# Sixteen products and their additions moved ahead of the edges in the last two row tiles of a four-layer graph kernel

## The chip, the cores and the metric

The kernel runs on one core of one Trainium2 chip. The metric is the device time of one execution in microseconds (us). The time before is the median of three runs, 1643.59 us (1642.99 to 1648.46).

The core has five engines that work side by side and wait for each other through semaphores: TensorE (PE, matrix products), VectorE (DVE), ScalarE (ACT), GpSimd (POOL) and SyncE (SP, which here only issues DMAs). SBUF is the on-chip memory, PSUM the small memory that TensorE writes its products to.

## What is computed

The input is a node matrix x of 4096 x 128 and a sparse weighted matrix adj of 4096 x 4096, both float32. Four graph layers follow each other, and each is a residual step with a layer norm:

```python
x = layernorm(x + L0(x, adj, W, a))        # signed attention
x = layernorm(x + L1(x, adj, W0, W1))      # Chebyshev convolution
x = layernorm(x + L2(x, adj, weight, ...)) # four attention heads
x = layernorm(x + L3(x, adj, W_self, W_neigh))

# L2: attention of each node over its entries of adj
C = alpha_src[None, :, :] + alpha_dst[:, None, :]
tau = adj.T[..., None] * exp(maximum(0.2 * C, C))
z = einsum('mnh,nhf->mhf', adj.T[..., None] * tau / tau.sum(1, keepdims=True), h_prime)

# L3: mean over neighbours
deg = clip(adj.sum(1, keepdims=True), 1.0)
out = h @ W_self + (adj @ h / deg) @ W_neigh
```

The change concerns the end of the kernel, where L2 and L3 run interleaved.

## The kernel before

The 4096 nodes are cut into 32 row tiles of 128 (t = 0 to 31) and into 8 column blocks of 512. In L2, adj is treated as a list: each node has a few non-zero entries, and for each row tile the rows of a table in device memory that these entries name are gathered by GpSimd's indirect DMAs, nine per tile (`gathers`, L1846). L3 treats adj as a dense matrix and streams its columns from device memory in chunks of 1 MB (`columns`, L1945, issued on SP's queue). Both are done in one loop over the row tiles (L2109 to L2134), so that a row tile that L2 has finished can enter L3 at once.

The order of the work on TensorE, VectorE, ScalarE and GpSimd is the order in which the program writes it (`manual_schedule`, L2009): no scheduler moves anything. What can be said early and done late is therefore written out by hand with two queues of generators. `pieces` holds L3's products, `chains` the steps that turn a finished row tile into L3's input. The steps of one row tile t in the loop are:

- `targets(t + 1)` (L1861): three small matmuls on TensorE for the next tile.
- `multiply(6)`: up to six products of L3. One product (L1957) is a matmul of 128 x 128 y by a 128 x 512 piece of the chunk; the products of one column block over the row tiles of a group add up in one PSUM bank of the pool "pp", which has four. When the last product of a block is written, the bank goes on the list `adds`. `multiply` stops as soon as four banks are on it.
- `edges(t)` (L1872 to L1884): the attention weights of L2, on VectorE, with one exponential on ScalarE (L1879). It needs the gathered rows.
- `add_up()` (L1970): VectorE adds every bank on `adds` to the running sum acc3 in SBUF, and so frees the banks.
- `sums` (L1889, L1890): four matmuls that add up the weighted rows. They need the results of `edges`.
- `multiply(2)`: two more products.
- `divide` (L1896 to L1898) and `turn` (L1907): the row tile is divided by its weights' sum, added to x and transposed on TensorE.
- When a group of row tiles is complete, `layer3_rows` (L1914 to L1933): ScalarE copies the transposed tile, TensorE multiplies it by L3's two weight matrices (L1924), and ScalarE scales the result to y (L1928) and to x (L1933). From then on the group's products are on `pieces`. Between its three steps stand single products.
- `gathers(t + 2)`: GpSimd's gathers for the tile after the next.

The groups have 1, 1, 2, 4, 4, 4, 4, 2, 2, 2, 2, 2, 1 and 1 row tiles. The last three are 28 and 29 together, 30, and 31. When t = 30 begins, the products of 28 and 29 (16 of them) are still to be done, and a few of the group before.

After the loop (L2135 to L2139) what is left on `pieces` is done, two products at a time with their additions. The products of row tile 31 are not on `pieces`: `layer3_end` (L1980, L1982) computes them while it transposes acc3 block by block, divides by the degree, normalizes (L1984 to L2006) and writes the output (L2007). The first L1982 needs y of row tile 31.

The core of the two helpers that the change calls:

```python
def multiply(n):
    for _ in range(n):
        if len(adds) > 3:
            break
        one(pieces)
```

Of the kernel before, what the change touches and what calls it, by code (L numbers as in the profile page):

```python
# [47 lines left out]
def adj_resnorm_d4(ctx: ExitStack, tc: tile.TileContext, x_in, xT_in, adj, adjT, pairs, diag_in, w0g, w0gT, a0, w1a, b1a,  # L48
# [9 lines left out]
    NT = N // P  # L58
# [623 lines left out]
    def network(usual):  # L682

        with ExitStack() as whole:
# [161 lines left out]
            if usual:  # L846
                sparse_layers(enter, lists, w, h0T)
                return
# [885 lines left out]
    def sparse_layers(enter, lists, w, h0T):  # L1734
# [103 lines left out]
        def gathers(t, behind={}):  # L1838
            if t >= NT:
                return  # L1840
            if t not in got:
                got[t] = l2.tile([P, E, F + H], F32, name="got", bufs=4)
            if 2 <= t < EARLY:
                nc.scalar.copy(got[t][:, 0:QT, :], packed[:, t - 2])
            for j in range(QT if t < EARLY else 0, E):
                nc.gpsimd.indirect_dma_start(got[t][:, j, :], None, table,  # L1846
                                             bass.IndirectOffsetOnAxis(ap=lists.source[:, t, j:j + 1], axis=0))
                if j % 2:
                    lists.pause(behind.get(j))

        def load_spread(c):
            if c < NB:
                wide[c] = l2.tile([P, TB, SLOTS], BF16, name="spread")
                nc.scalar.dma_start(wide[c].rearrange("p k s -> p (k s)"), spread[c])

        def targets(t):
            if t < NT:
                at = wide[t // TB][:, t % TB]
                told[t] = psum.tile([P, QT * W + E * H + F + H], F32, name="u")
                for j in range(QT):  # L1860
                    nc.tensor.matmul(told[t][:, j * W:(j + 1) * W], at[:, j * P:(j + 1) * P], dst[:, t], start=True, stop=True)  # L1861

        def edges(t):

            g, u = got.pop(t), told.pop(t)
            d = u[:, 0:QT * W].rearrange("p (j s) -> p j s", s=W)
            wt = u[:, QT * W:QT * W + E * H].rearrange("p (j h) -> p j h", h=H)
            a = lists.value[:, t][:, :, None].to_broadcast([P, E, H])
            gw = l2.tile([P, E + 1, F + H], F32, name="gw")
            nc.scalar.copy(gw[:, E, :], own[:, t, :])  # L1870
            into = l2.tile([P, QT, P], F32, name="into")
            nc.vector.tensor_tensor(into, lists.iota[:, None, :].to_broadcast([P, QT, P]),  # L1872
                                    d[:, :, 3 * H:W].to_broadcast([P, QT, P]), ALU.is_equal)
            e = l2.tile([P, E, H], F32, name="score")
            nc.vector.tensor_reduce(e[:, 0:QT], d[:, :, 0:3 * H].rearrange("p j (s h) -> p j h s", s=3), AX.X, ALU.add)
            nc.vector.tensor_tensor(e[:, QT:], g[:, QT:, F:F + H], near[:, t, :][:, None, :].to_broadcast([P, NEAR, H]), ALU.add)
            nc.vector.tensor_tensor(e[:, 0:QT], e[:, 0:QT], g[:, 0:QT, F:F + H], ALU.add)
            nc.vector.scalar_tensor_tensor(e, e, ALPHA, e, op0=ALU.mult, op1=ALU.max)
            nc.scalar.activation(e, e, AF.Exp)  # L1879
            nc.vector.tensor_tensor(gw[:, 0:E, F:F + H], e, a, ALU.mult)  # L1880
            nc.vector.tensor_tensor(wt, gw[:, 0:E, F:F + H], a, ALU.mult)
            nc.vector.tensor_tensor(heads(gw[:, 0:E, 0:F]), heads(g[:, :, 0:F]), wt[:, :, :, None].to_broadcast([P, E, H, FO]), ALU.mult)  # L1882
            here = l2.tile([P, F + H], F32, name="here")
            nc.vector.tensor_reduce(here, gw[:, QT:, :].rearrange("p j f -> p f j"), AX.X, ALU.add)  # L1884
            return u[:, QT * W + E * H:], into, gw, here

        def sums(so, into, gw, here):
            for j in range(QT):
                nc.tensor.matmul(so, into[:, j, :], gw[:, j, :], start=j == 0, stop=False)  # L1889
            nc.tensor.matmul(so, ident, here, start=False, stop=True)  # L1890
            return so

        def divide(t, so):
            rd = small.tile([P, H], F32, name="rd", bufs=3)
            z = l2.tile([P, 1, F], F32, name="z")
            nc.vector.reciprocal(rd, so[:, F:F + H])  # L1896
            nc.vector.tensor_tensor(heads(z), heads(so[:, None, 0:F]), rd[:, None, :, None].to_broadcast([P, 1, H, FO]), ALU.mult)
            nc.vector.tensor_add(x[:, t, :], z[:, 0, :], x[:, t, :])  # L1898
            return rd[:, 0:1]
# [3 lines left out]
        def turn(t, t0, n):  # L1903

            if t == t0:
                turned[t0] = ps_x.tile([P, n, P], F32, name="px")
            nc.tensor.transpose(turned[t0][:, t - t0, :], x[:, t, :], ident)  # L1907
            stats(x[:, t, :], t)

        def layer3_rows(t0, n):  # L1910

            s = small.tile([P, n], F32, name="rstd2")
            xb = l2.tile([P, n, P], F32, name="oT")
            nc.scalar.copy(xb, turned.pop(t0))  # L1914
            inverse(s, mv[:, t0:t0 + n, 1])
            nc.scalar.activation(warm, eps, AF.Exp)
            yield
            qs = []
            for k0 in range(0, n, 2):
                m = min(2, n - k0)  # L1920
                q = ps_x.tile([P, m, 2, F], F32, name="px")
                qs += [(k0 + k, q[:, k]) for k in range(m)]
                for k in range(m):
                    nc.tensor.matmul(q[:, k].rearrange("p s f -> p (s f)"), xb[:, k0 + k, :],  # L1924
                                     W3.rearrange("p s f -> p (s f)"), start=True, stop=True)
            yield
            for k, q in qs:
                nc.scalar.activation(y[:, t0 + k, 0:F - 1], q[:, 0, 0:F - 1], AF.Copy, scale=s[:, k:k + 1])  # L1928
            if t0 + n < NT:
                pieces.append(layer3_product(t0, n))  # L1930
                yield
            for k, q in qs:
                nc.scalar.activation(x[:, t0 + k, :], q[:, 1, :], AF.Copy, scale=s[:, k:k + 1])  # L1933
            yield
# [27 lines left out]
        def add_up():  # L1962
            while adds:
                t0, p, blk = adds.popleft()
                nonlocal summed
                summed = acc3[:, blk.start:blk.start + 1]
                if t0 == 0:
                    nc.scalar.copy(acc3[:, blk], p)
                else:
                    nc.vector.tensor_add(acc3[:, blk], p, acc3[:, blk])  # L1970
# [38 lines left out]
        with tc.manual_schedule(engines={mybir.EngineType.PE, mybir.EngineType.DVE, mybir.EngineType.Activation,  # L2009
# [3 lines left out]
            def one(queue, n=1):  # L2013
                while queue and n:
                    r = next(queue[0], queue)
                    if r is not queue:
                        n -= 1
                    else:
                        queue.popleft()
# [6 lines that stand above are left out]
# [83 lines left out]
            for t in range(NT):  # L2109
                t0, n = of[t]  # L2110
                if t % TB == 1:
                    load_spread(t // TB + 1)
                if t == 3:
                    lists.check(ps_x, "px")
                targets(t + 1)
                multiply(6)
                made = edges(t)
                add_up()
                one(chains)
                if t == t0 + n - 1:  # L2120
                    nc.scalar.activation(warm, eps, AF.Sqrt)
                so = sums(*made)
                multiply(2)
                rd = divide(t, so)
                turn(t, t0, n)
                if t == t0 + n - 1:
                    chains.append(layer3_rows(t0, n))
                for _ in range(3):
                    one(chains)
                    multiply(1)  # L2130
                behind = {1: rd}
                if summed is not None:
                    behind[5] = summed
                gathers(t + 2, behind)  # L2134
# [53 lines left out]
```

## Time and profile before

| | |
|---|---|
| Median of three runs | 1643.59 us (1642.99 to 1648.46) |
| Profiled execution | 1824.21 us, span from first to last instruction 1822.3 us |
| TensorE busy | 1538.9 us, 84% of the span |
| VectorE busy | 1140.9 us, 63% |
| GpSimd busy | 834.8 us, 46% |
| ScalarE busy | 387.1 us, 21% |
| 1755.23 to 1778.65 us of the span | TensorE busy 19.16 of 23.42, VectorE 15.95, ScalarE 8.28, GpSimd 4.87 |
| 1778.65 to 1791.53 us | TensorE busy 12.88 of 12.88, VectorE 7.72, ScalarE 1.39 |
| 1791.53 to 1822.3 us | TensorE busy 14.45 of 30.77, VectorE 18.80, ScalarE 18.09 |

The profile is of one execution with the hardware's profiler on, and that execution took 180.6 us longer than the median of the runs without it. Times of single events below are microseconds from the start of its span. In a timeline line the columns are: start, length, engine, line of the kernel, operation, what is written and read, shape, and the number of instructions merged into the line; a bracket at the end gives the idle time of the engine just before and what ended it ("issue" or "remote" where the profile shows nothing that ended it). A float32 product of L1957 appears as two matmul records. The ends of matmul records are modelled.

### The profile page before, as it was taken

How to read it: one execution, taken by the hardware profiler on the slowest of the kernel's cores; microseconds unless marked ns; L12 is line 12 of the kernel's file. 1: busy time of each engine (PE TensorE's matmuls, PEld its weight loads, DVE VectorE, ACT ScalarE, POOL GpSimd, SP SyncE). 2: the span in 40 equal slices, each digit the busy share in tenths (PEclk: the TensorE clock that was granted, in tenths of full speed). 3: DMA queues.
4: the chain of work that ended last, by engine and by line, in shares of the span. 5: the costliest groups of instructions: out<-in, count | busy, mean ns of one | idle time of the engine just before them, and what ended most of it. 6: DMA issues, size and time to landing. Idle time of an engine off the chain costs nothing.

```text
span 1822.3 us, 16500 instructions
## 1 busy us (share of the span) xinstructions
PE 1538.9 (84%) x4740; PEld 735.8 (40%) x4744; DVE 1140.9 (63%) x3209; ACT 387.1 (21%) x698; POOL 834.8 (46%) x1336
## 2 busy tenths in 40 slices
PE   6899999999999679887988968889936678878786
PEld 3344445444444224443444433444413334434334
DVE  5887647898878458764788920255426654545566
ACT  5766411100000101210200000023314111112224
POOL 0000000002423883364376784888485766766741
PEclk9899999999999779898999977999967788778988
DMA  9787675688898346563676836788864466556764
GB/s 383 290 311 263 235 259 193 245 320 307 294 340 305 115 164 237 185 222 137 206 265 220 298 95 226 264 278 286 286 165 127 162 220 226 195 194 219 223 178 110
DMA packets 111199, 421.47 MB, mean 231 GB/s; under 512 B 21685, under 2 KB 48314, under 8 KB 71290
## 3 DMA queue, kind: packets, MB, share of 16 engines
q1 hardware_dynamic: 59984, 360.01, 54.6%
q0 software_dynamic: 22656, 36.17, 8.0%
q10 hardware_dynamic: 28458, 24.14, 4.6%
q8 instruction: 39, 0.64, 0.1%
q14 instruction: 62, 0.51, 0.1%
HBM read 404.39 MB, written 15.86 MB: 231 GB/s over the span
## 4 chain that ended last, share of the span: by engine, by line
PE 49%; DVE 25%; issue 9%; another core or an unknown queue 8%; ACT 4%; DMA 3%; POOL 2%; ACTq 0%; DVEq 0%; POOLq 0%
PE pacc L731 17%; PE pacc L424 11%; PE pp L1957 6%; PE pp L2076 5%; DVE at L1403 2%; DVE top L1402 2%; DVE here L1884 2%; DVE here L1562 2%; DVE gw L1882 1%; DVE spread L1318 1%; DVE same L1318 1%; DVE acc L1970 1%; PE pden L412 1%; PE px L1924 1%
## 5 line engine op out<-in xcount | busy, mean ns | idle before, releaser
L1846 POOL DMA_INDIRECT got<-table,source x267 | 255.7, 958 | 69.3 <-issue 66.2
L1957 PE MATMUL pp<-chunk,xT 128*128 128x512 f32 x496 | 260.3, 668 | 8.1 <-ACT xT L1928 5.3
L1524 POOL DMA_INDIRECT got<-rows,source x180 | 182.7, 1015 | 123.6 <-DVE rec L1318 48.2
L731 PE MATMUL pacc<-chunk,x 128*128 128x512 f32 x512 | 222.7, 593 | 0.0
L731 PE MATMUL pacc<-chunk,t 128*128 128x512 f32 x384 | 187.9, 637 | 10.5 <-issue 10.5
L424 PE MATMUL pacc<-chunk,hw 128*128 128x512 f32 x408 | 190.7, 612 | 0.8 <-DVE hw L467 0.7
L2076 PE MATMUL pp<-chunk,w 128*128 128x512 f32 x384 | 172.1, 598 | 0.0
L731 PE MATMUL pacc<-chunk,v 128*128 128x512 f32 x320 | 154.5, 626 | 9.4 <-issue 9.3
L1360 POOL IOTA i<- 128x384 int32 (+3 forms) x4 | 0.9, 237 | 347.8 <-PE pden L412 330.7
L731 PEld LDWEIGHTS pacc<-chunk,x 128*128 128x128 f32 x512 | 96.1, 190 | 114.6 <-issue 114.6
L1957 PEld LDWEIGHTS pp<-chunk,xT 128*128 128x128 f32 x496 | 99.6, 215 | 104.9 <-issue 92.8
L1402 DVE MAX8 top<-chunk 128x8 f32<-128x512 f32 x196 | 128.5, 677 | 16.0 <-DMA chunk<-in_adjT 16.0
L1403 DVE FIND_INDEX8 at<-top,chunk 128x8 uint16<-128x512 f32 x196 | 133.1, 685 | 0.0
L731 PEld LDWEIGHTS pacc<-chunk,t 128*128 128x128 f32 x384 | 77.0, 206 | 104.1 <-issue 104.1
L1569 POOL TENSOR_TENSOR idle<-idle 128x1 f32<-128x1 f32 x508 | 114.1, 225 | 8.9
L1524 POOL DMA_INDIRECT both_ways<-in_pairs,both_at x108 | 105.3, 975 | 17.4 <-issue 17.3
L424 PEld LDWEIGHTS pacc<-chunk,hw 128*128 128x128 f32 x408 | 75.5, 193 | 92.8 <-issue 87.0
L396 ACT ACTIVATE junk<-chunk 128x2048 fp8e4<-128x2048 f32 x51 | 97.4, 1910 | 29.0 <-DMA chunk<-in_adjT 28.6
L2076 PEld LDWEIGHTS pp<-chunk,w 128*128 128x128 f32 x384 | 71.5, 193 | 78.5 <-issue 77.8
L330 DVE TENSOR_SCALAR pos<-chunk 128x2048 bf16<-128x2048 f32 x66 | 80.2, 1219 | 35.9 <-DMA chunk<-in_adjT 35.9
L1970 DVE TENSOR_TENSOR acc<-pp,acc 128x512 f32<-128x512 f32 x96 | 62.5, 683 | 61.2 <-remote 40.0
L731 PEld LDWEIGHTS pacc<-chunk,v 128*128 128x128 f32 x320 | 60.6, 198 | 83.5 <-issue 83.5
(433 smaller groups left out, 2063.6 us busy)
## 6 DMA issues: line engine op xcount, KB each, us to landing
chunk<-in_adjT SPq DMA_DIRECT2D x326, 1024.0 KB
keep<-in_adjT SPq DMA_DIRECT2D x13, 1024.0 KB
spread<-spread ACTq DMA_DIRECT2D x16, 384.0 KB
got<-table,source POOLq DMA_INDIRECT x267
chunk<-in_adjT ACTq DMA_DIRECT2D x4, 1024.0 KB
got<-rows,source POOLq DMA_INDIRECT x180
table<-rows ACTq DMA_DIRECT2D x8, 264.0 KB
xT<-in_xT ACTq DMA_DIRECT2D x8, 256.0 KB
```

Source lines behind the costliest of these rows:

```text
L330: r = nc.vector.tensor_scalar(pos, a, 0.0, None, op0=ALU.is_gt)
L396: nc.scalar.activation(junk, a, AF.Relu, scale=-1.0, accum_out=bad[:, n:n + 1], saturate=False)
L424: in_order(nc.tensor.matmul(p, hw[:, j * TB + k, :], a[:, k, :], start=first and k == 0, stop=last and k == TB - 1))
L731: nc.tensor.matmul(p, stationary(c * TB + k), a[:, k, :], start=n == 0 and k == 0, stop=n == NB - 1 and k == TB - 1)
L1402: pin(nc.vector.max(self.top[:, t, ib, :], row))
L1403: pin(nc.vector.max_index(self.at[:, t - TB, ib, :], self.top[:, t, ib, :], row))
L1524: tc.keep_in_program_order(nc.gpsimd.indirect_dma_start(out, None, of, bass.IndirectOffsetOnAxis(ap=index, axis=0)))
L1569: return nc.gpsimd.tensor_tensor(self.idle[:, 0:1], of, self.idle[:, 1:2], ALU.mult)
L1846: nc.gpsimd.indirect_dma_start(got[t][:, j, :], None, table, bass.IndirectOffsetOnAxis(ap=lists.source[:, t, j:j + 1], axis=0))
L1957: nc.tensor.matmul(p, y[:, t0 + k, :], a[:, ib % (TB // n), k, :], start=k == 0, stop=k == n - 1)
L1970: nc.vector.tensor_add(acc3[:, blk], p, acc3[:, blk])
L2076: nc.tensor.matmul(p, w[:, c * TB + k, :], a[:, k, :], start=n == 0 and k == 0, stop=n == NB - 1 and k == TB - 1)
```

## The change

In the iterations t = 30 and t = 31, after `multiply(6)` and ahead of `edges(t)`, the kernel now adds up the banks, does up to eight products, adds up, does up to eight products, and adds up. Nothing else is touched: the same products and additions are done in the same sequence among themselves. What they follow and precede on TensorE and VectorE is different.

```diff
                 targets(t + 1)
                 multiply(6)
+                if t >= NT - 2:
+                    for _ in range(2):
+                        add_up()
+                        multiply(8)
+                    add_up()
                 made = edges(t)
                 add_up()
                 one(chains)
```

`multiply(8)` stops at four full banks. A product of the group of 28 and 29 fills half a bank's sum, so eight of them fill four banks. A product of t = 30 alone completes one.

## The prediction

> **What bounds the kernel now.** The edit touches only the last two row tiles (t = 30 and t = 31) of the last loop, so I read the end of the kernel: the chain of waits in order of time, then the timelines of TensorE, VectorE and ScalarE from 1735 us on. The chain's columns are start, length, and what ran.
>
> ```profile
> 1754.12 4.33 issue
> 1758.45 0.62 ACT xT L1928 x2
> ...
> 1761.29 1.82 DVE here L1884
> ...
> 1763.96 3.56 PE pp L1957 x4
> ...
> 1778.82 12.87 PE pp L1957 x30
> ```
>
> The last stall before the close is ScalarE's 4.33 us ahead of L1928 (it makes y of row tiles 28 and 29). Then edges, sums and products alternate, and from 1778.82 to 1791.7 TensorE alone sets the time: fifteen products (two records each) that had been left over. These are what the edit moves forward.
>
> TensorE's timeline:
>
> ```profile
> 1752.46 1.13 PE L1924 MATMUL px<-W,oT 128*128 128x256 f32 x4 [1.19 <-issue]
> ...
> 1755.23 2.82 PE L1957 MATMUL pp<-chunk,xT 128*128 128x512 f32 x6
> 1761.31 1.69 PE L1889 MATMUL u<-gw,into 128*128 128x132 f32 x6 [3.26 <-issue]
> ...
> 1763.76 3.77 PE L1957 MATMUL pp<-chunk,xT 128*128 128x512 f32 x4
> 1767.33 0.31 PE L1907 MATMUL px<-ident,x 128*128 128x128 f32 x1
> ...
> 1773.06 0.84 PE L1889 MATMUL u<-gw,into 128*128 128x132 f32 x6
> ...
> 1778.65 13.04 PE L1957 MATMUL pp<-chunk,xT 128*128 128x512 f32 x30
> ```
>
> Between 1755.23 and 1791.53 TensorE idles 4.3 us (busy 19.16 of the first 23.42 us, then all of 12.88), nearly all in two places: 3.26 us ahead of the sums of t = 30, and 0.64 us before a turn. The fifteen products at the end run back to back at 0.858 us each (12.87 / 15).
>
> VectorE's timeline:
>
> ```profile
> 1740.99 0.52 DVE L1872 TENSOR_TENSOR into<-iota,u 128x384 f32<-128x384 f32 x1
> ...
> 1744.21 1.82 DVE L1884 TENSOR_REDUCE here<-gw 128x132 f32<-128x924 f32 x1
> ...
> 1759.43 0.20 DVE L1880 TENSOR_TENSOR gw<-score,value 128x36 f32<-128x36 f32 x1 [5.63 <-ACT score L1879]
> ...
> 1763.02 2.47 DVE L1970 TENSOR_TENSOR acc<-pp,acc 128x512 f32<-128x512 f32 x4
> ```
>
> An undisturbed edges step (t = 29, first two lines) takes 5.04 us from the start of L1872 to the end of L1884. That of t = 30 is broken by a wait of 5.63 us for ScalarE.
>
> **What the Trainium skill says.** "TensorE: Matmul & The Clock Gate", Part 1, "What's actually happening": after an idle window of about 3.4 us the array runs at half rate, until about 3.4 us of activity. The trace agrees: after the 3.26 us idle two products took 3.77 us, and the two after t = 31's sums, with no such idle, 1.98. The same page, Part 3, "The mechanism": matmuls start and end in program order; Part 1, "Architectural detail", says strict first-in first-out for VectorE and ScalarE. So what is put ahead really holds what follows. "Perfetto Trace Analysis", "Tensor Engine Instruction (MATMUL, LD_WEIGHTS)": a matmul's recorded end is an estimate, and others are told only when PSUM has acknowledged. Here that gap is large: L1924 ends by record at 1753.6, but L1928, which waits for it, starts at 1758.45; a column load on SP's queue that waits for the product recorded to end near 1756.3 was issued at 1763.4.
>
> **The change, part by part.** Counts are read from the built programs' order. Nothing is added or removed: the same 29 products from here to the end, the same additions, DMAs and transposes. What moves: ahead of the sums of t = 30 stand 19 products instead of 3, and ahead of its edges on VectorE 12 additions, of which 4 stood just after them and 8 come from later. Between L1924 of tile 30 and the sums of t = 31 stand 8 products instead of 5, and ahead of the edges of t = 31 9 additions that stood after them. None is left after t = 31, so the 12.87 us at the end go. SP keeps its order of column loads; five chunk buffers rotate, each load waits for the products that free its buffer, and those come earlier now. The gathers on POOL were issued for t = 31 in the iteration of t = 29 (last one at 1760.08), so they pass nothing that moved.
>
> What the move breaks is the overlap. In the kernel before, VectorE does edges while TensorE does products. Now the products of t = 30 come first, with VectorE idle apart from additions, and then the edges, with TensorE idle. The new path, from 1755.23, when the three old products start:
>
> 1. 19 products x 0.858 = 16.3.
> 2. The last addition, 0.69 + 0.03 = 0.7. Only then do t = 30's edges start.
> 3. Edges, 5.04. The 5.63 us wait for ScalarE is gone, as L1928 has run long before.
> 4. From the end of L1884 over the sums, divide and two products to the turn L1907: 4.2 as at t = 30 before (1763.11 to 1767.33) with the slow clock; 2.0 with the fast one. I count 2.0 here and the rest under "slow clock".
> 5. Turn to y of tile 30: 1767.33 to 1769.90 before, 2.6 (a table load of 1.28 is in it).
> 6. Its 8 products x 0.858 = 6.9. They read that y, so they cannot start earlier.
> 7. The last addition 0.7, then t = 31's edges 5.0.
> 8. Sums, divide, turn 1.7; turn to y of tile 31 2.6. The closing matmuls L1982 need this y. Before, it was ready at 1779.8 and hidden under the fifteen products; with that cover gone it counts.
>
> Sum 16.3 + 0.7 + 5.0 + 2.0 + 2.6 + 6.9 + 5.7 + 4.3 = 43.5 us, against 36.3 before (1755.23 to 1791.53, the first L1980): **+7.2 us**.
>
> Then three terms whose size the trace does not give for the new order:
>
> - Slow clock after idle. TensorE now idles 5 us ahead of each sums step. Ahead of t = 30's: 4.2 - 2.0 = 2.2. Ahead of the close: eight 128-column matmuls of a block took 1.9 us, at half rate 3.8, and part of the second block is slow too: 0 to 4. I take 2.2 + 2.
> - Late completions. Additions 2 to 4 of t = 30 must see their products before products reuse the four "pp" banks. If they become visible only at 1763.4, as they did before, the fifth new product starts at 1764.2 in place of 1761.5: 0 to 2.9. I take 1.5.
> - Column loads: the new order needs four 1 MB chunks in 13.7 us. Three had been issued by 1751.4, the fourth by 1763.4 for use at about 1770; cost 0, up to 3 if it lands late. Below nothing none of these terms goes, since each only adds waiting.
>
> Total 7.2 + 2.2 + 2 + 1.5 = 12.9 us. It is a difference inside the profiled execution, which took 1824.21 us (span 1822.3), while the median run is 1643.59, 11% less. The instructions at the end are of fixed length, so I carry microseconds over, not percent: 1643.6 + 12.9 = **1656.5 us**.
>
> **The rivals.**
>
> *The stalls of before belong to the profiled execution.* If completions come promptly in the timed runs, the kernel before needs only TensorE's own time in that stretch: 24.9 for products and about 4.2 for two tiles' sums, turns and L1924, 29.1 in place of 36.3. The new path, serial anyway, keeps 43.5 + 4.2. Then the change costs 18.6: about 1662. For it: the profiled execution is 180 us longer. Against it: the waits recur in every group of two tiles (at 1729.99 too), and POOL's pace would then hold the kernel before back.
>
> *The moved work fills a wait for gathers, and the kernel is not slower.* One place: L1876, where edges wait for the gathered rows of t = 30 and t = 31. POOL issues one gather per 1.3 us (seven from 1751.94 to 1761.05), so 11.7 us per tile; VectorE needs about 9.2 (edges 5.0, four additions 2.5, divide and statistics 1.7). If the timed runs are bound by POOL, edges of t = 31 wait about 4 us and those of t = 30 about 2.5, in which the moved products are free. It decides once the two waits together exceed the 12.9. Then the kernel would be at 1643 or, with 5 us more of waiting, 1638. Against it: in the last two tiles the trace has no wait for a gather at all; the longest near the end is 2.51 us, at t = 26, and POOL itself waits 4.2 us in every second tile for VectorE.
>
> *TensorE's clock stays up and completions are prompt only in the new kernel.* Then only 7.2 is left: 1650.8, still slower.
>
> **How the numbers follow.** A difference of 0.3%, 4.9 us, is about what a measurement of this kernel can tell. The forecast, serial path with 7 to 16 us, gets 0.72 (the third case is its lower end); prompt completions in the timed runs, 16 to 21 us, 0.14; gathers that hide it 0.14, half of it within 0.3% and half faster. Slower is 0.72 + 0.14 = 0.86. The range goes from 1649.5, under the third case, to 1663, over the first rival; it leaves out the gathers' case, and little above. The likeliest case's own range is 1650.5 to 1660.
>
> **What would show it.** In the changed kernel's timeline: 38 product records in one run before t = 30's sums, then TensorE idle for 4 to 5 us ahead of L1889 of t = 30 and again of t = 31; a turn of tile 31 followed directly by L1980 and L1982, with no product between; VectorE's L1872 of t = 30 right after the twelfth addition. The wait at L1880 of t = 30 falls from 5.63 us to about 0.3. From the first product of t = 30 to the first L1984 it should take 48 to 52 us in place of 38.3. I am wrong if edges of t = 30 or t = 31 wait for gathers by more than 5 us in either kernel's timed execution, if TensorE stays busy through the edges, or if the close starts within 38 us of the first product.

## The result and the profile after

The changed kernel takes 1656.95 us (median of six runs, 1654.58 to 1659.92). In the same group of runs the kernel before takes 1647.0 us (six runs, 1642.99 to 1650.0). The ratio is 1.0066, with a 95% interval from 1.0046 to 1.0086: slower by 10.0 us, between 7.6 and 14.2. The forecast was 1656.5 us, made from 1643.6 plus 12.9.

In one of the four groups of runs (`no_last_add`, `warm`, `overlap_28` and `overlap_all` below) the kernel before itself took 1830.81 us, 11% longer than in the others and like the execution behind the profile shown ahead of the prediction; times of that group are compared only within it.

The traces below set the change against a second profile of the unchanged kernel, from an execution of 1647.67 us; it is the experiment `before_again`. First the busy time by stretch: from the first product of t = 30 to the first L1984, and from there to the end. The columns are the stretch, its length, the busy time with the number of instructions of TensorE, of its weight loads, of VectorE, ScalarE and GpSimd, then TensorE's granted clock, DMA share and GB/s. The changed kernel:

```profile
1576.08:1626.49 50.41, 38.22 (x102) 19.45 (x101) 24.91 (x49) 9.06 (x21) 8.38 (x12) 0.83 0.54 129
1626.49:1655.30 28.81, 12.47 (x112) 12.28 (x110) 18.07 (x116) 18.09 (x73) 4.76 (x8) 0.78 0.25 77
```

The kernel before, the same two stretches:

```profile
1578.51:1616.99 38.48, 33.66 (x102) 17.32 (x101) 24.91 (x49) 8.96 (x21) 8.39 (x12) 0.91 0.70 170
1616.99:1645.90 28.91, 12.47 (x112) 12.28 (x110) 18.08 (x116) 18.09 (x73) 4.76 (x8) 0.75 0.25 77
```

All of the loss lies in the first stretch, 50.41 against 38.48 us, or 11.9 us; the close is the same to 0.1 us. Instruction counts are equal (102 on TensorE, 49 on VectorE), and VectorE is busy for the same 24.91 us. TensorE does the same work in 4.6 us more (38.22 against 33.66, at a lower mean clock) and idles for 12.2 us in place of 4.8. That 11.9 in the traces is 10.0 between the medians is within the scatter: the six runs of each kernel spread over 5.3 and 7.0 us, and ahead of this stretch, where both programs have the same order of instructions, the two executions differ by 2.4 us (1576.08 against 1578.51).

The chain of waits of the changed kernel (start, length, what ran), which in the kernel before ended in thirty product records, now goes over edges and sums to the end:

```profile
1585.08 8.21 DMA got<-table,source
1593.29 0.53 DVE into L1872
...
1596.52 1.82 DVE here L1884
...
1604.63 8.85 PE pp L1957 x16
...
1617.35 1.83 DVE here L1884
```

The first of these lines misleads: the chain puts the start of the edges of t = 30 down to a gather. The one issued at 1585.08 is the last of all, so it belongs to t = 31, whose edges come 20 us later, and VectorE's timeline further below shows that it reaches L1872 without idling. TensorE's timeline of the changed kernel:

```profile
1576.08 16.55 PE L1957 MATMUL pp<-chunk,xT 128*128 128x512 f32 x38
1596.54 1.69 PE L1889 MATMUL u<-gw,into 128*128 128x132 f32 x6 [3.90 <-DVE gw L1882]
...
1604.63 8.83 PE L1957 MATMUL pp<-chunk,xT 128*128 128x512 f32 x16 [1.26 <-ACT xT L1928]
1617.37 0.94 PE L1889 MATMUL u<-gw,into 128*128 128x132 f32 x6 [3.91 <-DVE gw L1882]
...
1623.81 0.79 PE L1982 MATMUL pp<-xT,chunk 128*128 128x128 f32 x2 [0.31 <-ACT xT L1928]
```

Thirty-eight records run without a break, then TensorE waits 3.90 us for edges; sixteen records, then 3.91 us for edges again. VectorE's timeline of the changed kernel shows why the edges are late:

```profile
1592.67 0.69 DVE L1970 TENSOR_TENSOR acc<-pp,acc 128x512 f32<-128x512 f32 x1 [1.02 <-PE pp L1957]
1593.28 0.54 DVE L1872 TENSOR_TENSOR into<-iota,u 128x384 f32<-128x384 f32 x1
...
1613.50 0.69 DVE L1970 TENSOR_TENSOR acc<-pp,acc 128x512 f32<-128x512 f32 x1 [0.17 <-PE pp L1957]
1614.11 0.54 DVE L1872 TENSOR_TENSOR into<-iota,u 128x384 f32<-128x384 f32 x1
```

L1872 of t = 30 starts right behind the twelfth addition, which waited for the nineteenth product. That is 17.20 us after the first product (1593.28 - 1576.08). The next line of t = 30 that needs gathered rows, L1876, starts at 1593.85 without a wait. The edges of t = 31 in the same way start behind the last addition of tile 30's products.

### The profile page after: what moved, and what is told of

Read it like the earlier page. It is cut to its first block, busy times and chain, and to the rows that moved or that the text cites. A ratio compares the mean times of both kernels' runs of the same rounds, so it can differ in the third digit from the quotient of the medians.

```text
span 1655.3 us, 16507 instructions
## 1 busy us (share of the span) xinstructions
PE 1478.9 (89%) x4740; PEld 715.9 (43%) x4744; DVE 1139.1 (69%) x3209; ACT 387.8 (23%) x698; POOL 837.0 (51%) x1336
## 4 chain that ended last, share of the span: by engine, by line
PE 42%; DVE 26%; POOL 15%; DMA 7%; issue 6%; ACT 3%; ACTq 0%; DVEq 0%; POOLq 0%
PE pacc L731 15%; PE pacc L424 12%; POOL got L1846 6%; POOL got L1524 4%; PE pp L1957 3%; PE pp L2076 3%; DMA got<-table,source 3%; DVE at L1403 3%; DVE top L1402 3%; POOL idle L1569 2%; DVE gw L1882 1%; DVE here L1884 1%; POOL value L1524 1%; DVE same L1318 1%; DVE here L1562 1%
## 5 line engine op out<-in xcount | busy, mean ns | idle before, releaser
L1957 PE MATMUL pp<-chunk,xT 128*128 128x512 f32 x496 | 244.2, 636 | 2.2 <-ACT xT L1928 2.0
L731 PE MATMUL pacc<-chunk,t 128*128 128x512 f32 x384 | 171.3, 597 | 0.0
L731 PE MATMUL pacc<-chunk,v 128*128 128x512 f32 x320 | 144.5, 597 | 0.0
L1957 PEld LDWEIGHTS pp<-chunk,xT 128*128 128x128 f32 x496 | 95.2, 205 | 95.8 <-issue 88.4
L731 PEld LDWEIGHTS pacc<-chunk,t 128*128 128x128 f32 x384 | 71.7, 192 | 81.7 <-issue 81.7
L1889 PE MATMUL u<-gw,into 128*128 128x132 f32 x192 | 34.4, 325 | 71.3 <-DVE gw L1882 71.3
```

The lines of the kernel that those rows point to most:

```text
L731: nc.tensor.matmul(p, stationary(c * TB + k), a[:, k, :], start=n == 0 and k == 0, stop=n == NB - 1 and k == TB - 1)
L1957: nc.tensor.matmul(p, y[:, t0 + k, :], a[:, ib % (TB // n), k, :], start=k == 0, stop=k == n - 1)
```

## The experiments

My theory: the loss is lost overlap, because the additions that now stand ahead of the edges wait for products, and so put the edges behind those products; part of it is the slow clock after TensorE's waits. The rivals: TensorE's own order (19 products ahead of the sums) costs, whatever VectorE does; or waits in the kernel before, for gathers above all, set the size.

### before_again: what the kernel before waits for

The kernel before, unchanged.

> The kernel before, unchanged, for a second profile of it, since the profiled execution on record took 180 us more than the timed runs. Ratio 1.00 within 0.2%. From the start of the three products of t = 30 (L1957 just after L1861) to the first L1984 the changed kernel takes 50.4 us. Lost overlap as the cause: about 40 us here (50.4 less the 10 us by which the medians differ), with VectorE in edges and TensorE in products at the same time. If the late completions of the first profile belong to the kernel and not to that one execution, ScalarE again waits over 4 us ahead of L1928 of tiles 28 and 29, and the stretch is again 38 us; if they belong to that execution, L1928 follows L1916 at once. Rival of the gathers: edges of t = 30 wait at L1876 or L1877 for a gather; from the changed kernel's trace (gathers for t = 30 issued to the end at 1574.4, landing some 3 us later) I expect 3 us of wait at t = 30 and about 2 us at t = 31.

Measured: 1646.29 us, ratio 0.9998 (0.9982 to 1.0014); stretch 38.48 us. VectorE's timeline of this execution, L1876 of t = 28 to 31, the first instruction of the edges that needs gathered rows:

```profile
1558.16 0.18 DVE L1876 TENSOR_TENSOR score<-got,near 128x24 f32<-128x24 f32 x1 [5.21 <-DMA got<-table,source]
...
1566.97 0.17 DVE L1876 TENSOR_TENSOR score<-got,near 128x24 f32<-128x24 f32 x1
...
1582.43 0.18 DVE L1876 TENSOR_TENSOR score<-got,near 128x24 f32<-128x24 f32 x1 [5.92 <-DMA got<-table,source]
...
1592.28 0.17 DVE L1876 TENSOR_TENSOR score<-got,near 128x24 f32<-128x24 f32 x1
```

TensorE's timeline of the same execution:

```profile
1585.15 1.69 PE L1889 MATMUL u<-gw,into 128*128 128x132 f32 x6 [3.82 <-DVE gw L1882]
...
1587.60 3.41 PE L1957 MATMUL pp<-chunk,xT 128*128 128x512 f32 x4
...
1602.13 13.04 PE L1957 MATMUL pp<-chunk,xT 128*128 128x512 f32 x30
```

The stretch is as long as in the first profile (38.3 us), but for another reason. ScalarE is not late: its L1928 of tiles 28 and 29 starts at 1577.18, 0.30 us after the recorded end of L1924, where the first profile had 4.9. VectorE waits 5.92 us for the gathers of t = 30 and not at all for those of t = 31 (3 and 2 us were expected), TensorE therefore waits 3.82 us, and two products then take 3.41 us in place of 1.9. In this case's other execution with untouched edges of t = 30, `t31_only`, that wait is 5.29 us. So the gathers' rival had its mechanism: in the changed kernel, where products and additions stand in this place, the wait is gone.

### t30_only and t31_only: each tile alone

The change made in one of the two tiles only (the second one has `NT - 1`):

```diff
-                if t >= NT - 2:
+                if t == NT - 2:
```

> The moved products and additions in row tile 30 alone (the condition is t == NT - 2): 19 products ahead of the sums of t = 30 and 12 additions ahead of its edges, as in the change; t = 31 as in the kernel before, so that edges of t = 31 run beside products. Lost overlap as the cause, one edges step of about 5 us plus its slow clock instead of two: edges of t = 31 no longer wait for the eight products of tile 30 (8.8 us in the changed kernel), first L1984 about 8 us earlier than in the changed kernel: 1647 + 2.5, ratio 1.0015 (1.000 to 1.003). Rival, the products ahead of the sums of t = 30 on TensorE are the cost whatever VectorE does: 16 of the 19 moved products are moved here too, so nearly the whole cost stays, ratio 1.005 to 1.006.

> The change in row tile 31 alone (t == NT - 1): t = 30 as before, 18 products in place of 5 ahead of the sums of t = 31, 12 additions ahead of its edges. Lost overlap: one edges step behind the products. Products end about when they ended before less the sums and turns that now follow; after them 0.7 + 5.0 + 1.9 + 2.6 us instead of nothing, less the 12.9 - 1.7 us of tail that were moved: 1647 + 3, ratio 1.002 (1.000 to 1.005). Rival, the number of moved products counts: 13 of 16, ratio about 1.005.

Measured: `t30_only` 1649.23 us, 1.0017 (1.0005 to 1.0029), stretch 41.26 us, +2.8. `t31_only` 1650.45 us, 1.0028 (1.0014 to 1.0041), stretch 43.41 us, +4.9. TensorE's timeline of `t30_only`, the sums of t = 31:

```profile
1617.20 0.84 PE L1889 MATMUL u<-gw,into 128*128 128x132 f32 x6
```

And of `t31_only`, the same step:

```profile
1610.54 1.54 PE L1889 MATMUL u<-gw,into 128*128 128x132 f32 x6 [3.91 <-DVE gw L1882]
```

The wait of 3.9 us stands in the tile that was changed (in `t30_only` ahead of the sums of t = 30, 3.90 us). In `t30_only` the edges of t = 31 still run beside products, and the sums of t = 31 wait for nothing. The two alone make 2.8 + 4.9 = 7.7 us, less than the whole 11.9. A reading that fits, but that no run isolates: each tile alone leaves products to run beside the other's edges, and both together leave none.

### no_last_add and no_last_add_b: TensorE's order kept, one addition step fewer

TensorE's order is exactly that of the change; only the last `add_up()` of the added lines is gone, so that VectorE has eight additions instead of twelve ahead of the edges of t = 30, and eight instead of nine ahead of those of t = 31.

```diff
                 if t >= NT - 2:
                     for _ in range(2):
                         add_up()
                         multiply(8)
-                    add_up()
```

> The change without its last addition step: TensorE's order is the same as in the changed kernel, 19 products ahead of the sums of t = 30 and 8 ahead of those of t = 31; only on VectorE four additions of t = 30 and one of t = 31 stand after the edges instead of ahead of them. Edges of t = 30 then wait for 11 products instead of 19. If additions ahead of the edges are the cause (lost overlap): edges of t = 30 start 10.2 us after the first product instead of 17.2, end beside the last products, TensorE has no idle ahead of the sums of t = 30, its clock stays up; the stretch from the first product to the first L1984 falls from 50.4 to about 41 us: ratio 1.0008 (0.9990 to 1.0025). Rival, the products' place on TensorE is the cost: nothing changes, ratio 1.0066.

> The same kernel as no_last_add, again: the change without its last addition step, so that TensorE's order is that of the change and VectorE has eight additions instead of twelve ahead of the edges of t = 30, and eight instead of nine ahead of those of t = 31. With products' ends seen promptly, my theory (the edges start too late because the additions ahead of them wait for products) expects the edges of t = 30 to run beside the last eight products, about 6.5 us earlier than in the change, those of t = 31 one product earlier, and no slow clock ahead of the sums of t = 30: a stretch of 40 to 43 us and 1.001 to 1.003. The rival, that TensorE's order itself costs (19 products ahead of the sums), expects 1.006 as in the change.

Measured: `no_last_add_b` 1647.8 us, 1.0015 (1.0002 to 1.0028), stretch 41.61 us (1581.79 to 1623.40). `no_last_add`, against 1830.81 us, took 1838.04 us, 1.0038 (1.0014 to 1.0062), more than expected; its stretch was 47.0 us. VectorE's timeline of `no_last_add_b`, the start of the edges of t = 30:

```profile
1592.19 0.54 DVE L1872 TENSOR_TENSOR into<-iota,u 128x384 f32<-128x384 f32 x1
```

And its TensorE:

```profile
1581.79 16.55 PE L1957 MATMUL pp<-chunk,xT 128*128 128x512 f32 x38
1598.18 0.84 PE L1889 MATMUL u<-gw,into 128*128 128x132 f32 x6
...
1603.39 7.13 PE L1957 MATMUL pp<-chunk,xT 128*128 128x512 f32 x16 [1.27 <-ACT xT L1928]
1613.56 0.94 PE L1889 MATMUL u<-gw,into 128*128 128x132 f32 x6 [3.04 <-DVE gw L1882]
```

The same 38 records run in the same 16.55 us, but the edges of t = 30 start 10.40 us after the first product instead of 17.20, beside the last products. (They start 2.7 us after the last gather's issue at 1589.51, in the changed kernel 8.2 us after it; so it was not the gathers that held the edges there.) The sums follow without a wait and at full clock, and the sixteen records take 7.13 us instead of 8.83. The stretch is 8.8 us shorter than the change's (50.41 - 41.61); the median is 1.8 us above that of the kernel before in the same group, in place of 10.0. So TensorE's order is cleared of three quarters of the loss: it is the last addition step, five additions in all, that costs. What is left, 3.1 us of the stretch, is a balance: at t = 31 no product remains to run beside the edges (3.04 us of waiting, and slow matmuls in the close), while the 3.82 us that the kernel before waited at t = 30 are gone.

### warm and warm_b: the price of the slow clock

The change, with four more products per tile that only keep TensorE busy during the edges; nothing reads what they write.

```diff
                     add_up()
+                    idle = ps_p.tile([P, IB], F32, name="pp")
+                    for _ in range(4):
+                        nc.tensor.matmul(idle, ident, acc3[:, 0:IB], start=True, stop=True)
```

> The changed kernel with four additional float32 matmuls of 128 x 512 after the last addition step of t = 30 and of t = 31, whose result nobody reads: 3.4 us of TensorE's work in the 3.9 us in which it waits for the edges. It only keeps the array busy. If the slow clock is worth what the trace of the changed kernel shows (1.7 us from the edges' end to the turn of t = 30, 2.0 in the eight products of tile 30, some 0.7 in the close), the stretch falls by 4.4 us to 46 and the ratio to 1.0040 (1.003 to 1.005). If the slow clock were the main cost, the ratio falls to 1.001 or less; if it costs nothing, it stays at 1.0066 or rises.

> The same kernel as warm, again: the change, with four more products ahead of each of the two sums steps, whose results nothing reads; they only keep TensorE busy while VectorE does the edges. If the slow clock after the idle stretches is worth what I gave it, about 2.2 us at t = 30 and 2 us at the products of tile 30, the stretch falls from 50.4 to about 46.5 us and the time is 1.003 to 1.004. If the slow clock is hidden behind other waits, it stays at 1.0065.

Measured: `warm_b` 1654.86 us, 1.0053 (1.0032 to 1.0073), stretch 47.50 us (1580.75 to 1628.25). `warm`, against 1830.81 us, took 1844.38 us, 1.0070 (1.0043 to 1.0098). The timed difference from the change (1.0066) is too small to tell, so a gain in time is not shown; the trace is what counts here. TensorE's timeline of `warm_b`, where L2124 is the filler:

```profile
1597.14 3.60 PE L2124 MATMUL pp<-acc,ident 128*128 128x512 f32 x8
1601.20 0.94 PE L1889 MATMUL u<-gw,into 128*128 128x132 f32 x6 [0.47 <-DVE gw L1882]
...
1607.69 7.13 PE L1957 MATMUL pp<-chunk,xT 128*128 128x512 f32 x16 [1.26 <-ACT xT L1928]
```

With the wait cut from 3.90 to 0.47 us, the way from the end of L1884 of t = 30 (1603.00) to its turn (1605.10) takes 2.10 us in place of 3.71, and the eight products of tile 30 take 7.13 us in place of 8.83. The turn of t = 31 follows 0.31 us sooner. That is 3.6 us gained; the close gives 0.7 back, since its first matmuls run slow all the same, and for longer. The stretch is shorter by 2.9, about 4 were expected. This agrees with the Trainium skill, "TensorE: Matmul & The Clock Gate", Part 1, "What's actually happening", which has the clock halved after an idle window of about 3.4 us.

### overlap and overlap_b: products ahead, nothing behind them

Only the first half of the change: one addition step to free the banks, eight products, and then the edges at once.

```diff
                 if t >= NT - 2:
-                    for _ in range(2):
-                        add_up()
-                        multiply(8)
-                    add_up()
+                    add_up()
+                    multiply(8)
```

> In row tiles 30 and 31 one addition step and then up to eight products, and no additions after them ahead of the edges: 11 products in place of 3 ahead of the sums of t = 30, 10 in place of 5 ahead of those of t = 31, but only four additions ahead of each edges step, of products that stand before. So thirteen products are moved forward on TensorE, and the edges on VectorE do not wait for any of them; 2 products are left after t = 31 instead of 15. Lost overlap as the cause: the edges run beside the eight products, TensorE has no idle of 4 us ahead of the sums, and the tail is shorter by 13 x 0.858 = 11 us, of which some 7 us come back as later sums: about 1647 - 4, ratio 0.9975 (0.995 to 1.000). Rival, products ahead of the sums on TensorE are the cost: still slower than before, ratio 1.003 or more. Rival, slow clock alone: no idle, so about the ratio of the first.

> The same kernel as overlap, again: one addition step and eight products ahead of the edges of t = 30 and t = 31, no addition after them. My theory (products beside edges cost nothing and shorten the end; only the additions ahead of the edges cost) expects 0.996 of the kernel before again, if products' ends are seen promptly (stretch of about 32 us in place of 38.5). If they are seen late, as in the last four runs, the first addition step waits for them and the edges with it: then 1.000 to 1.004. The rival, that the first run of overlap was luck, expects 1.000 with a stretch of 38 us.

Measured: `overlap` 1638.51 us, 0.9959 (0.9944 to 0.9974); `overlap_b` 1638.38 us, 0.9948 (0.9929 to 0.9966). It beats both kernels, in two groups of runs. The stretch is 32.12 and 32.10 us. TensorE's timeline of `overlap_b` (the lines are the products ahead of the sums of t = 30, these sums, the products ahead of the sums of t = 31, and the last products):

```profile
1578.53 9.69 PE L1957 MATMUL pp<-chunk,xT 128*128 128x512 f32 x22
1588.05 0.84 PE L1889 MATMUL u<-gw,into 128*128 128x132 f32 x6
...
1592.07 8.75 PE L1957 MATMUL pp<-chunk,xT 128*128 128x512 f32 x20
...
1606.93 1.88 PE L1957 MATMUL pp<-chunk,xT 128*128 128x512 f32 x4
```

Both sums steps (those of t = 31 at 1600.65) start straight after products, at full clock, and four records are left at the end in place of thirty. The edges of t = 30 start 3.53 us after the first product (L1872 at 1582.06) and run beside the next products.

One thing stays open. In these two executions the gathers were further ahead: GpSimd issued the last one at 1580.94 and 1582.00, against 1587.53 in `before_again`, and the wait for gathers fell in t = 29 (6.01 and 6.12 us) instead of t = 30. The gathers of t = 30 had all been issued by 1571.4 in `overlap_b`, 7 us ahead of the first product, and L1876 of t = 30 waits for nothing; so no wait for gathers was filled here. In the stretch of `overlap_b` TensorE is busy for 30.56 us and idle for 1.5, in `before_again` 33.66 and 4.8: the 6.4 us between them are the wait ahead of the sums of t = 30 and the slow matmuls after it. A kernel before that met the gathers so early would have neither, and by these numbers (an estimate) would need about 32 us too. And from the issue of the last gather, which the edit does not move, to the end of the span both executions take 57.4 us, `before_again` 58.4. The gain in the medians, 7.0 and 7.6 us, is measured; that it comes from the products beside the edges, and not from another placing of the waits, the traces do not show.

### overlap_28, overlap_28_b and overlap_all: the same in more tiles

`NT - 4` in place of `NT - 2` in `overlap` (t = 28 to 31); in `overlap_all` no condition at all:

```diff
-                if t >= NT - 2:
-                    add_up()
-                    multiply(8)
+                add_up()
+                multiply(8)
```

> One addition step and up to eight products ahead of the edges, none after them, in the last four row tiles instead of the last two. In the kernel with two tiles TensorE still idles 4.0 us ahead of the sums of t = 28, where the edges wait 6.0 us for a gather, and nothing of that size later. If work moved under such a wait is free as long as the edges do not wait for it, 2 to 4 us more are won: ratio 0.9945 (0.992 to 0.997). If the moved products are then missing in t = 30 and 31, where no tail is left to shorten, it is as the kernel with two tiles, 0.996.

> The same kernel as overlap_28, again: overlap also in t = 28 and t = 29. With products' ends seen promptly the gather wait of 6 us that overlap still has at t = 28 leaves time for products: 0.993 to 0.997 if they fill it, at best 3 us under overlap. If the products that t = 28 would take are simply missing later, the same as overlap, 0.996. If the additions ahead of the edges of t = 28 hold the edges up and with them the next gathers, over 1.000.

> The same in every row tile. Before t = 28 the gathers set the pace of the loop, so products moved there fill TensorE's waits and the total of its idle stays: the same as with four tiles, ratio 0.9945 (0.991 to 0.998). If additions ahead of the edges cost in every tile, it is slower than that, up to 1.00.

Measured: `overlap_28_b` 1650.61 us, 1.0030 (1.0016 to 1.0045). Against 1830.81 us, `overlap_28` took 1837.94 us, 1.0044 (1.0024 to 1.0064), and `overlap_all` 1877.37 us, 1.0248 (1.0210 to 1.0286). The gain that was expected of `overlap_28` and `overlap_all` did not come. VectorE's timeline of `overlap_28_b`, L1876 of t = 28, 29 and 30:

```profile
1558.40 0.18 DVE L1876 TENSOR_TENSOR score<-got,near 128x24 f32<-128x24 f32 x1
...
1573.23 0.17 DVE L1876 TENSOR_TENSOR score<-got,near 128x24 f32<-128x24 f32 x1
...
1592.32 0.17 DVE L1876 TENSOR_TENSOR score<-got,near 128x24 f32<-128x24 f32 x1
```

And its TensorE between t = 29 and t = 30:

```profile
1575.93 0.94 PE L1889 MATMUL u<-gw,into 128*128 128x132 f32 x6 [2.19 <-DVE gw L1882]
...
1579.31 0.47 PE L1907 MATMUL px<-ident,x 128*128 128x128 f32 x1 [0.93 <-DVE x L1898]
```

From the edges of t = 28 to those of t = 29 it takes 14.8 us (1573.23 - 1558.40), in `before_again` 8.8: additions that wait for the extra products stand ahead of them. Then the products have run out: no L1957 stands between the sums of t = 29 and y of tiles 28 and 29, and TensorE waits at every step. From t = 28 to t = 30 it takes 33.9 us in place of 24.3, to t = 31 (1607.00) 48.6 in place of 34.1, and the fewer products at the end give only a part of this back: to the first L1984 it takes 62.5 us in place of 58.8. In this execution the products moved into t = 28 and 29 met no wait for gathers to fill, and the later tiles missed them.

In `overlap_all` VectorE's additions wait long for products (engine, what waited, for what: us in total, times, longest):

```profile
DVE acc L1970 <- PE pp L1957: 94.2, 30, 19.9
```

How much of this is the additional addition step in every tile, and how much that products' ends were seen late in executions of that length, was not separated.

## Why the prediction was right

The verdict and the size were forecast, and the path was the predicted one. Step by step, in the changed kernel's own trace:

| step of the prediction | forecast | measured, and from what |
|---|---|---|
| 1 and 2, nineteen products and the last addition | 17.0 | 17.20 (1576.08 to 1593.28) |
| 3, edges of t = 30 | 5.04 | 5.05 (to 1598.33, the end of L1884) |
| 4, to the turn, with the slow clock | 2.0 + 2.2 | 3.71 (to 1602.04) |
| 5, to y of tile 30 | 2.6 | 2.59 (to 1604.63) |
| 6, its eight products | 6.9 | 8.87 (to 1613.50) |
| 7, addition and edges of t = 31 | 5.7 | 5.67 (to 1619.17) |
| 8, sums, divide, turn; then y of tile 31 | 1.7 + 2.6 | 1.88 + 2.76 (to 1623.81) |
| from the closing matmuls to the first L1984 | 2.0 + 2 | 2.68 (to 1626.49) |

*The serial path* (steps 1 to 8, "VectorE idle apart from additions, and then the edges, with TensorE idle") was right to within 0.2 us at each step outside the slow clock. What I did not see is that it hangs for the most part on the last addition step: I priced that step at 0.7 us and its five additions' place at nothing of its own, while `no_last_add_b` shows that with it gone 8.8 of the 11.9 us go.

*Slow clock*: forecast 2.2 + 2. The sum was about right, the place of the second part was not. Measured against `warm_b` and `before_again`: 1.6 us ahead of the turn of t = 30, 1.7 in the eight products of tile 30, which I had priced at full clock, 0.3 ahead of the turn of t = 31, and 0.9 in the close (2.68 from its first L1982, against 1.76), together 4.5.

*Late completions*: forecast 1.5, measured 0 here. The 38 records ran without a break. (The upper end of 2.9 does not follow from the 1764.2 and 1761.5 given for it, which are 2.7 apart.) In `no_last_add`, an execution of 1834.41 us, the effect is there: VectorE's timeline has this wait ahead of the second of the additions that now precede the edges of t = 30:

```profile
1760.08 0.69 DVE L1970 TENSOR_TENSOR acc<-pp,acc 128x512 f32<-128x512 f32 x1 [5.11 <-PE pp L1957]
```

so that term belongs to executions like the profiled one of 1824.21 us, and I had carried it over to the timed ones.

*Column loads*: forecast 0, measured 0; no product waits for a chunk.

The stretch was forecast at 36.3 + 2.0 + 12.9 = 51.2 us and measured at 50.41; against 38.48 before, 11.9 in place of 12.9. The median came 0.5 us from the forecast partly by luck: the kernel before had a median 3.4 us above the three runs that I started from, and the difference of medians was 10.0.

*The rivals.* The first (the stalls of before belong to the profiled execution, +18.6) was half right: ScalarE's 4.3 us stall and the 5.63 us wait at L1880 are not in `before_again`. But the 5.92 us wait for gathers stands in the same place, so the stretch before is as long. That GpSimd's pace would hold the kernel before back was argued; that one wait replaces the other to within 0.2 us (38.28 and 38.48) is luck. Without any such wait the stretch before would be about 32 us, as estimated from `overlap_b`, and the change would lose some 18 us, as this rival said. The second (gathers hide the change) had the right mechanism, which I set aside because "in the last two tiles the trace has no wait for a gather at all". That was true of the one execution that I had, and false of `before_again` and `t31_only`. It did not decide, as the waits of both tiles were 5.92 + 0 us, under the 12.9 that it needs. My own criterion, that I am wrong if edges wait for gathers by more than 5 us, was met without making the forecast wrong: a wait of nearly that length, for ScalarE, was already in the sum. The third (clock stays up, +7.2) is refuted by the slow sums and products.

## What to carry to other kernels

When work of an in-order queue is moved ahead of a critical step, look at what comes with it on the other engines: products moved ahead on TensorE cost little here, but an addition on VectorE that must wait for the last of them puts the critical edges behind all of them. Free the buffers, issue the products, and let the step that others wait for go next; leave collecting the results for afterwards. In the last two tiles that order was faster than the kernel before; in four, or in all, it was slower. And where a stall will be filled, check in more than one execution that it is there, and stop moving work when later tiles would run out of it.

## What the hardware showed that was not expected

- The same program waited very differently in its two profiles. In the one of 1824.21 us two of VectorE's waits read:

```profile
DVE acc L1970 <- remote: 40.0, 10, 7.4
DVE acc L1970 <- PE pp L1957: 13.7, 16, 2.9
```

  In `before_again` the same additions wait 6.6 us in all and at most 1.0 us at once. What makes the difference was not found.
- The close of `warm_b` ran slow (two L1924 records in 1.22 us, against 0.59 in `before_again`) though TensorE had no single wait over 1.1 us there: 0.47, 0.91, 1.01 and 0.35 us between small matmuls were enough.
- Which tile waits for its gathers is not fixed by the order of the work: t = 28 and t = 30 wait in `before_again` (5.21 and 5.92 us), t = 28 and not t = 29 also in the profile of the change (5.17 us), but t = 29 in `overlap` and `overlap_b` (6.01 and 6.12 us, t = 28 under 1.7), although all these programs say the same up to t = 30. Whether this is chance or goes with the program is open.
